# Two GNN layers on 4096 nodes: layer 0 from block sums of h by mask matmuls, lists and gathers only for edges that share a block

## The chip, the cores and the metric

The kernel runs on one core of a Trainium2 chip. The metric is the device time of one execution in microseconds (us); lower is better. Fourteen executions of the kernel before gave a median of 809.99 us, from 802.71 to 822.25 us. The engines are named as in the profile: PE (TensorE matmuls), PEld (TensorE weight loads, which overlap PE), DVE (VectorE), ACT (ScalarE), POOL (GpSimd), SP (SyncE, which here only issues transfers).

## What is computed

`x` is 4096 x 64 and `adj` a 4096 x 4096 matrix of zeros and ones, one entry in 512 set. Two layers follow each other, cut here to what matters:

```python
def logmap(x, y):                      # Poincare ball, c = 1
    sub = mobius_add(-x, y)            # a fraction in x, y and their dot products
    return 2 / lam(x) * arctanh(clip(norm(sub))) * sub / norm(sub)

h = relu(layernorm(x))
w = adj / deg                          # deg: row sums of adj
agg = einsum('ij,ijc->ic', w, logmap(h[:, None], h[None, :]))
x = x + expmap(0, agg @ W0 + b0)       # layer 0

h = relu(layernorm(x))
support = h @ W1
rank = cumsum(adj, axis=1); deg = rank[:, -1:]; k = minimum(deg, 100)
pos = rank - (deg - k)
w = adj * where(pos > 0, 0.5 ** (k - pos), 0)
x = x + w @ support + b1               # layer 1
```

Layer 0 weighs each edge (i, j) by a function of the squared distance of h_i and h_j, so it needs both rows for each edge. Layer 1 weighs the n-th edge of a row, counted from the right, by 2^-n.

## The kernel before

**Blocks.** The 4096 rows are 32 row blocks of 128 (NB = 32). Four quarters q hold eight row blocks each (QB = 8). The 4096 columns are 32 column blocks of 128. `load` (L814) brings a quarter of a row block, 128 x 1024 f32 or 512 KB, into a tile `a_sb` (three buffers), transposes it on PE by eight 128 x 128 matmuls (L821), and ACT writes it as an 8-bit mask into `masks[q]` (L823), which stays on the chip.

**Layer 0.** Each row has some eight edges. `pack` (L831) multiplies each 128 x 128 mask by an 8-column matrix `pk` (L845), so that every row gets 256 numbers, each of which encodes 16 columns. `search` (L858) takes the 24 largest of them with MAX8 and MATCH_REPLACE8. The first eight become lists of edges of the row itself (`ell_lists`, ELL = 8). What is over goes through `tail_split`, `tail_first` and `tail_second` (L889 to L994): edges of eight rows, then of a whole row block, are merged through DRAM tables `tl_d` and `ta_d` into lists that any row may own (TB = 2 a row block and partition), with the owner's number in `tail_r`. This happens once for each quarter. `gather` (L1006) fetches one h row for each partition with one indirect DMA of POOL: 256 for the row's own lists and 64 for the merged ones, 320 in all. `tail_rows` (L1022) makes one-hot matrices on POOL (L1031) and, by matmuls, the owners' rows. `differ`, `weigh`, `total` and `total_tail` (L1052 to L1145) compute differences, weights and sums on DVE and ACT. They run in 16 units of two row blocks; units 4 to 15 have some merged lists too. The sums are `st["y", q]`, from a pool of three buffers.

**Between the layers.** `middle` (L1163) finishes layer 0 for a group of row blocks and makes the support rows and their differences, split in three bf16 parts (`sup`).

**Layer 1.** `suffix` (L1254) and `ranks` (L1264) turn the masks into the powers of two. `collect` (L1288) multiplies them with `sup`: 33 blocks for each of 32 row blocks, 128 x 192 matmuls, in five sums (`sums`, L811), each added to `acc` by DVE (L1304, L1308).

**Order.** The program is written as a plan: `at(when, fn, ...)` gives each step a time in us, `EARLY` (L806) moves most steps but not the loads by 20 or 30 us ahead, and the result is a priority. A scheduler in the compiler orders each engine's queue from the priorities and its own estimates, and the engines run their queues in that order. The plan's lines for the lists are

```python
t = loaded(q * QB + QB - 1) + 6.0
at(t, tail_split, q)
at(t + 12.0, tail_first, q)
at(t + 20.0, tail_second, q)
```

If a list overflows, a flag is set and a slow second program (`dense_path`) runs after this one.

Of the kernel before, what the change touches and what calls it, by code (L numbers as in the profile page):

```python
# [11 lines left out]
F32 = mybir.dt.float32  # L12
# [7 lines left out]
P = 128  # L20
# [29 lines left out]
QB = 8  # L50
GRP = 16
CAND = 24
ELL = 8
EXTRA = 8
RUN = 8
TAILW = CAND - ELL + EXTRA
SUB = 40
REST = 64
TB = 2
MAXT = 3  # L60
# [484 lines left out]
def kernel(  # L545
# [37 lines left out]
    NSL = 2 * ELL + MAXT * TB  # L583
# [9 lines left out]
    hp_d = dram.tile([N, 3 * DT], BF16, name="hp_d")  # L593
# [7 lines left out]
    with ExitStack() as fast:  # L601
# [46 lines left out]
        pk = const.tile([P, GB], BF16, name="pk")  # L648
        nc.vector.tensor_scalar(pk, gm, pw_i.bitcast(F32), None, ALU.mult)
        gn = const.tile([1, NG], BF16, name="gn")  # L650
# [4 lines left out]

        row_b = const.tile([P, 1], F32, name="row_b")
# [3 lines left out]
        full = const.tile([P, NQ, 6], F32, name="full")  # L660
# [5 lines left out]
        ell_v = const.tile([P, NB, ELL], F32, name="ell_v")  # L666
        ell_i = const.tile([P, NB, ELL], I32, name="ell_i")
# [72 lines left out]
        nc.vector.tensor_copy(gn, gn_i)  # L740
# [44 lines left out]
        hp = masks[NQ - 2].bitcast(BF16).rearrange("p b c -> p (b c)")[:, 0 : NB * 3 * DT]  # L785
        hp = hp.rearrange("p (b n c) -> p b n c", n=3, c=DT)
        for n in range(3):
            nc.vector.tensor_copy(hp[:, :, n, :], tab)
            if n < 2:
                nc.vector.tensor_tensor(tab, tab, hp[:, :, n, :], ALU.subtract)  # L790
        nc.sync.dma_start(out=by_rows(hp_d), in_=hp.rearrange("p b n c -> p b (n c)"))

        gp = fast.enter_context(tc.tile_pool(name="gp", bufs=2))
        blk = fast.enter_context(tc.tile_pool(name="blk", bufs=1))
        blk2 = fast.enter_context(tc.tile_pool(name="blk2", bufs=2))
        yp = fast.enter_context(tc.tile_pool(name="yp", bufs=3))
# [3 lines left out]
        ps_w = fast.enter_context(tc.tile_pool(name="ps_w", bufs=1, space=PSUM))  # L800
        ps_t = fast.enter_context(tc.tile_pool(name="ps_t", bufs=1, space=PSUM))
        ps_o = fast.enter_context(tc.tile_pool(name="ps_o", bufs=1, space=PSUM))
        ps_s = fast.enter_context(tc.tile_pool(name="ps_s", bufs=1, space=PSUM))
        ps_m = fast.enter_context(tc.tile_pool(name="ps_m", bufs=1, space=PSUM))

        EARLY = {"middle":30,"search":30,"fetch_words":30,"tail_rows":30,"differ":30,"weigh":30,"total":30,"total_tail":30,"ell_lists":30,"tail_split":20,"tail_first":20,"tail_second":20,"gather":30,"fetch":30}  # L806
# [4 lines left out]
        sums = [range(0, 8), range(8, 16), range(16, 24), range(25, 30), (24, 30, 31, None)]  # L811
# [19 lines left out]
        def pack(rb, n):  # L831

            q, b = divmod(rb, QB)
            if n == 0 and rb % 2 == 0:
                st["words", rb // 2] = ps_w.tile([P, 2, NG], F32, name="words")
                nc.tensor.matmul(
                    st["words", rb // 2].rearrange("p k g -> p (k g)"),
                    lhsT=ones_r,
                    rhs=gn.unsqueeze(1).to_broadcast([1, 2, NG]),
                    start=True,  # L840
                    stop=True,
                )
            words = st["words", rb // 2]
            for j in range(RUN * n, RUN * n + RUN):
                nc.tensor.matmul(  # L845
                    words[:, rb % 2, bass.ts(j, GB)],
                    lhsT=masks[q][:, j, bass.ts(b, P)],
                    rhs=pk,
                    start=False,
                    stop=True,  # L850
                    skip_group_check=True,
                )

        def fetch_words(rb):
            st["wsb", rb // 2] = lst.tile([P, 2, NG], F32, name="wsb")
            nc.scalar.copy(st["wsb", rb // 2], st["words", rb // 2])  # L856

        def search(rb):  # L858
# [4 lines left out]
            src = st["wsb", rb // 2][:, rb % 2, :]  # L863
# [8 lines left out]
        def ell_lists(rb, nb):  # L872

            q, b = divmod(rb, QB)
            w = st["cand", q][:, b : b + nb, 0:ELL]
            r2 = slice(rb, rb + nb)
            ci = lst.tile([P, 4, ELL], I32, name="ci4")[:, 0:nb]
            e = lst.tile([P, 4, ELL], I32, name="e4")[:, 0:nb]
            kk = lst.tile([P, 4, ELL], F32, name="kk4")[:, 0:nb]
            t = lst.tile([P, 4, ELL], F32, name="t4")[:, 0:nb]  # L880
            nc.vector.tensor_copy(ci, w)
            nc.vector.tensor_scalar(ci, ci, NG - 1, None, ALU.bitwise_and)
            nc.vector.tensor_scalar(e, w.bitcast(I32), 23, None, ALU.logical_shift_right)
            nc.vector.tensor_scalar(kk, e, -135.0, float(NG), ALU.add, ALU.mult)
            nc.vector.scalar_tensor_tensor(t, kk, 1.0, ci, ALU.add, ALU.add)
            nc.vector.scalar_tensor_tensor(ell_v[:, r2], kk, 0.0, t, ALU.is_ge, ALU.mult)
            nc.vector.tensor_scalar(ell_i[:, r2], ell_v[:, r2], -1.0, 0.0, ALU.add, ALU.max)

        def tail_split(q):  # L889

            cand = st["cand", q]
# [559 lines left out]
```

## Time and profile before

| | |
|---|---|
| median of 14 runs | 809.99 us |
| the profiled execution | 811.75 us, its span 810.0 us |
| PE / PEld busy | 391.7 / 322.7 us |
| DVE busy | 486.0 us in 1635 instructions |
| ACT busy | 237.8 us |
| POOL busy | 394.8 us in 396 instructions |
| HBM read | 84.12 MB |
| granted TensorE clock, mean | 0.681 |

Busy is the time in which an engine had at least one instruction under way. A group's line has, after the count, its busy time, the mean of one instruction in ns, and the idle time of the engine just before such instructions with what ended it; "issue" there is time in which the engine waited for nothing that the profile shows. The granted clock is the share of TensorE's clock that the throttle gave, 1.0 being full. "PE a_ps L821 x8" is a stretch of eight instructions on that engine, writing that tile, of that line of the program.

### The profile page before, as it was taken

The numbers are of one execution on the slowest core, as the hardware profiler recorded it, in microseconds if no ns is written. First come the engines' busy times: TensorE is split into PE (matmuls) and PEld (weight loads), VectorE is DVE, ScalarE is ACT, GpSimd is POOL, SyncE is SP. The second block draws the span as 40 slices with busy tenths as digits, with TensorE's granted clock in tenths as the row PEclk, the third lists the DMA queues.
The fourth block names the chain that finished last, engine by engine and source line by source line (L and its number), as shares of the span: only waits on it lengthen the run. The fifth ranks groups of instructions, "written<-read, shape, count | busy, mean of one in ns | idle before, by whom it ended". The sixth has DMA issues, their size and how long they took to land.

```text
span 810.0 us, 10724 instructions
## 1 busy us (share of the span) xinstructions
PE 391.7 (48%) x3768; PEld 322.7 (40%) x3768; DVE 486.0 (60%) x1635; ACT 237.8 (29%) x335; POOL 394.8 (49%) x396
## 2 busy tenths in 40 slices
PE   4751227662753734212445548045136646468395
PEld 3640215451542522111235448033126545368284
DVE  5552139953984756775363336089936437569696
ACT  4640227752761614101211225025020102112100
POOL 0057472734187373277875642743858670741000
PEclk9999999755575555555556757555555959579598
DMA  7893447984884752011113448340211210100001
GB/s 243 273 347 104 116 137 240 294 252 123 261 258 130 246 162 58 18 31 30 32 29 93 101 124 258 67 105 13 34 22 32 31 22 12 26 13 3 0 2 56
DMA packets 49617, 89.11 MB, mean 110 GB/s; under 512 B 23571, under 2 KB 26899, under 8 KB 49299
## 3 DMA queue, kind: packets, MB, share of 16 engines
q1 hardware_dynamic: 32786, 74.93, 28.6%
q0 software_dynamic: 10240, 10.67, 8.9%
q10 hardware_dynamic: 6528, 2.75, 1.4%
q8 instruction: 31, 0.51, 0.3%
q14 instruction: 32, 0.25, 0.1%
HBM read 84.12 MB, written 4.19 MB: 109 GB/s over the span
## 4 chain that ended last, share of the span: by engine, by line
DVE 20%; PE 18%; another core or an unknown queue 16%; DMA 15%; issue 11%; POOL 11%; ACT 6%; SPq 1%; ACTq 0%; DVEq 0%; POOLq 0%
DMA a_sb<-in_adj 12%; POOL g L1014 8%; PE a_ps L1296 7%; PE a_ps L821 6%; ACT mask L823 3%; DVE red L1304 3%; POOL oh L1031 2%; DVE mask L1258 2%; PE words L1158 2%; DVE d L1089 1%; DVE acc L1308 1%; DVE d L1055 1%; PE sel L1124 1%; PE words L845 1%
## 5 line engine op out<-in xcount | busy, mean ns | idle before, releaser
L1014 POOL DMA_INDIRECT g<-tab_d,ell_i x256 | 278.5, 1088 | 288.6 <-issue 71.9
L823 ACT ACTIVATE mask<-a_ps 128x1024 fp8e5<-128x1024 bf16 x128 | 129.6, 1024 | 229.8 <-remote 116.8
L821 PE MATMUL a_ps<-ident_b,a_sb 128*128 128x128 bf16 x1024 | 129.3, 300 | 68.5 <-DMA a_sb<-in_adj 48.5
L821 PEld LDWEIGHTS <-a_sb 128*128 128x128 bf16 x1024 | 102.7, 162 | 83.4 <-DMA a_sb<-in_adj 61.6
L1296 PE MATMUL a_ps<-sup,mask 128*128 128x192 bf16 x1024 | 110.5, 267 | 36.0 <-issue 19.3
L1296 PEld LDWEIGHTS <-mask 128*128 128x128 fp8e5 x1024 | 97.5, 107 | 44.5 <-issue 41.4
L845 PE MATMUL words<-pk,mask 128*128 128x8 bf16 x1024 | 49.1, 171 | 112.0 <-ACT mask L823 77.3
L845 PEld LDWEIGHTS <-mask 128*128 128x128 fp8e5 x1024 | 43.2, 107 | 142.1 <-ACT mask L823 84.3
L1304 DVE TENSOR_REDUCE red<-a_ps 128x128 f32<-128x384 f32 x80 | 44.4, 555 | 70.1 <-remote 49.1
L1014 POOL DMA_INDIRECT g<-tab_d,tail_i x64 | 63.2, 987 | 18.4 <-issue 18.2
L1031 POOL TENSOR_SCALAR oh<-row,tail_r 128x128 bf16<-128x128 bf16 x64 | 51.3, 816 | 29.8 <-DVE r L1130 29.5
L1258 DVE TENSOR_TENSOR mask<-mask 128x512 int16<-128x512 int16 x112 | 43.1, 417 | 32.6 <-PE a_ps L821 19.8
L866 DVE MAX8 cand<-wsb 128x8 f32<-128x256 f32 x96 | 36.4, 413 | 33.5 <-ACT wsb L856 25.3
L1124 PE MATMUL sel<-d,mr 128*128 128x65 f32 x128 | 28.4, 392 | 52.1 <-issue 31.3
L1124 PEld LDWEIGHTS sel<-d,mr 128*128 128x128 f32 x128 | 26.9, 306 | 55.2 <-issue 51.0
L1089 DVE TENSOR_REDUCE d<-g 128x22 f32<-128x1408 f32 (+2 forms) x16 | 23.7, 1481 | 27.9 <-ACT g L1077 26.9
L1284 DVE TENSOR_TENSOR mask<-base,mask 128x4096 int16<-128x4096 int16 x16 | 36.5, 2280 | 5.0 <-ACT base L1280 5.0
L1036 PE MATMUL mi<-ident_b,oh 128*128 128x128 bf16 x64 | 13.7, 271 | 50.0 <-POOL oh L1031 37.8
L1154 PE MATMUL o<-ext,y 128*64 128x128 f32 x64 | 15.6, 384 | 40.6 <-DVE y L696 19.6
L1158 PE MATMUL words<-w_sb,a_sb 64*128 64x64 f32 x128 | 28.4, 388 | 10.0 <-ACT a_sb L1155 6.7
L1158 PEld LDWEIGHTS words<-w_sb,a_sb 64*128 64x128 f32 x128 | 25.3, 290 | 15.8 <-ACT a_sb L1155 10.2
L1155 ACT COPY a_sb<-o 64x512 f32<-64x512 f32 (+1 forms) x18 | 9.6, 532 | 74.1 <-PE o L1154 56.6
(310 smaller groups left out, 600.9 us busy)
## 6 DMA issues: line engine op xcount, KB each, us to landing
a_sb<-in_adj SPq DMA_DIRECT2D x128, 512.0 KB
g<-tab_d,ell_i POOLq DMA_INDIRECT x256
hp_d<-mask SPq DMA_DIRECT2D x1, 1560.0 KB
hr<-hp_d ACTq DMA_DIRECT2D x8, 146.2 KB
tab_d<-mask SPq DMA_DIRECT2D x1, 1040.0 KB
mask<-in_x SPq DMA_DIRECT2D x1, 1024.0 KB
hi<-tab_d ACTq DMA_DIRECT2D x16, 64.0 KB
g<-tab_d,tail_i POOLq DMA_INDIRECT x64
```

Of the source, the lines that this page charges most:

```text
L821: nc.tensor.transpose(a_ps[:, l, :], upper[:, l, :], ident_b)
L823: nc.scalar.activation(masks[q][:, bass.ts(n, RUN), bass.ts(b, P)], a_ps, AF.Copy, scale=2.0**-ONE_SHIFT, saturate=False,)
L845: nc.tensor.matmul(words[:, rb % 2, bass.ts(j, GB)], lhsT=masks[q][:, j, bass.ts(b, P)], rhs=pk, start=False, stop=True, skip_group_check= ...
L866: nc.vector.max(out=top, in_=src)
L1014: nc.gpsimd.indirect_dma_start(out=g[:, k, :], out_offset=None, in_=tab_d, in_offset=bass.IndirectOffsetOnAxis(ap=i, axis=0),)
L1031: nc.gpsimd.tensor_scalar(oh[:, k, :], row128, row[:, k : k + 1], None, ALU.is_equal)
L1124: nc.tensor.matmul(ag[:, k // TB, :], lhsT=mr[:, k, :], rhs=d[:, E2 + k, :], start=(k % TB == 0), stop=(k % TB == TB - 1),)
L1158: nc.tensor.matmul(sp[:, k, :], lhsT=ht[:, bass.ts(k, P)], rhs=w_sb, start=True, stop=True)
L1258: nc.vector.tensor_tensor(w[:, l, :], w[:, l, :], w[:, l + 1, :], ALU.add)
L1284: nc.vector.tensor_tensor(w, base.bitcast(I16).unsqueeze(1).to_broadcast([P, RUN, QR // 2]), w, ALU.subtract)
L1296: nc.tensor.matmul(o[:, k, :], lhsT=final if b is None else masks[p][:, b, rows], rhs=st["sup", c][:, j, :], start=(j == 0), stop=(j == nb ...
L1304: nc.vector.tensor_reduce(red, o.rearrange("p k (n c) -> p k c n", n=3), AX.X, ALU.add)
```

## The change

Layer 0 no longer lists every edge. Two column blocks of 128 make one "entry" of 256 columns (NE = 16 entries a row). `pack` now multiplies each mask by 12 columns (the eight of before, a count, and three parts of a scalar of the row) and, by three matmuls of 64 columns, by the three bf16 parts of h, summed over an entry in PSUM. Where a row has exactly one edge in an entry the sum is that edge's h; `differ`, `square`, `weigh` and `total` take all 16 entries of each row. Entries with two or more edges get weight zero (`entries`), and only their words are kept for `search`, which now takes 16; these edges alone go through the merged lists, TB = 4 a row block and partition, so 128 gathers, and `tail_rows` and `total_tail` work by row block, with the one-hot matrices made on DVE and not on POOL. The product with the weights in `total` is on POOL. The three parts of h stay on the chip (`hp`, in a constant tile that later holds `sup`). In layer 1 the first three sums become one of 24 blocks, and the support rows go through DRAM (`sup_d`, `differences`). `ranks` works on halves. The PSUM tiles are dealt out anew, the pool of `y` has two buffers and that of `D`, the differences of a row block, three. `EARLY` is empty, and the plan has new times. The units are 20: 16 of two row blocks, of which unit n >= 4 also has the merged lists of row blocks 2(n-4) and 2(n-4)+1, and four that have lists alone.

```diff
-CAND = 24
-ELL = 8
+CAND = 16
...
-SUB = 40
+PAIR = 2
+SIDE = 12
+SUB = 56
+DEAL = 8
-TB = 2
+TB = 4
...
-        gp = fast.enter_context(tc.tile_pool(name="gp", bufs=2))
+        gp = fast.enter_context(tc.tile_pool(name="gp", bufs=1))
+        dp = fast.enter_context(tc.tile_pool(name="dp", bufs=3))
+        sqp = fast.enter_context(tc.tile_pool(name="sqp", bufs=1))
-        yp = fast.enter_context(tc.tile_pool(name="yp", bufs=3))
+        yp = fast.enter_context(tc.tile_pool(name="yp", bufs=2))
+        ps_g = fast.enter_context(tc.tile_pool(name="ps_g", bufs=2, space=PSUM))
...
-        sums = [range(0, 8), range(8, 16), range(16, 24), range(25, 30), (24, 30, 31, None)]
+        sums = [range(0, 24), range(25, 30), (24, 30, 31, None)]
...
             for j in range(RUN * n, RUN * n + RUN):
+                at = masks[q][:, j, bass.ts(b, P)]
                 nc.tensor.matmul(
-                    words[:, rb % 2, bass.ts(j, GB)],
-                    lhsT=masks[q][:, j, bass.ts(b, P)],
-                    rhs=pk,
+                    st["words", rb][:, j, :], lhsT=at, rhs=side[:, j, :],
...
+                for t in range(3):
+                    nc.tensor.matmul(
+                        st["g", rb, hf][:, j // PAIR - hf * HE, :], lhsT=at, rhs=hp[:, j, t, 1:DT],
...
+        def entries(u):
+            nc.vector.tensor_tensor(cf, sv[:, :, 0, 0], sv[:, :, 1, 0], ALU.add)
+            nc.vector.tensor_reduce(we, sv[:, :, :, 1:], AX.XY, ALU.add)
...
+            nc.vector.scalar_tensor_tensor(we, cf, 1.5, we, ALU.is_lt, ALU.mult)
+            nc.vector.tensor_reduce(deg[:, rb : rb + 2], cnt, AX.X, ALU.add)
...
+            nc.vector.tensor_tensor(words, words, cols(mf, PAIR * GB), ALU.mult)
...
         def tail_second(q):
-            for k in range(4):
-                nc.sync.dma_start(
+            for k in range(DEAL):
+                for o in range(2):
+                    nc.sync.dma_start(out=dst[o], in_=src[o, DEAL - 1 - k if o else k])
...
-        def tail_rows(u):
-                nc.gpsimd.tensor_scalar(
+        def tail_rows(u, b):
+            for k in range(TB):
+                nc.vector.tensor_scalar(
                     oh[:, k, :], row128, tail_r[:, rb, k : k + 1], None, ALU.is_equal
...
+        def differ(u, b, hf):
+            if hf == 0:
+                u["D", b] = dp.tile([P, NE, D], F32, name="D")
             nc.vector.tensor_tensor(
+                u["D", b][:, hf * HE : (hf + 1) * HE, :],
+                st["g", rb, hf],
+                u["hi"][:, b, :].unsqueeze(1).to_broadcast([P, HE, D]),
                 ALU.subtract,
...
+        def square(u, b):
+                sq = sqp.tile([P, NE, D], F32, name="sq")
+                nc.scalar.activation(sq, u["D", b], AF.Square)
+                nc.vector.tensor_reduce(u["d2"][:, b * NE : (b + 1) * NE], sq, AX.X, ALU.add)
...
         def total(u):
+            for k in range(2):
+                dk = u["D", k]
+                nc.gpsimd.tensor_tensor(dk, dk, cols(r[:, k * NE : (k + 1) * NE]), ALU.mult)
+                nc.vector.tensor_reduce(
+                    y[:, b + k, 0:D], dk.rearrange("p e c -> p c e"), AX.X, ALU.add
...
+        def total_tail(u, b):
+            for k in range(TB):
+                nc.vector.tensor_scalar(
+                    mr[:, k, :], row128, tail_r[:, rb, k : k + 1], r[:, k : k + 1],
+                    ALU.is_equal, ALU.mult,
...
+        def differences(c, s):
+            if c == 0:
+                nc.sync.dma_start(out=dd[:, 1 : n + 1, :], in_=own)
+                nc.sync.dma_start(out=dd[:, 0:1, :], in_=prev[:, 0:1, :])
...
-        T0, TLOAD = 6.0, 8.4
+        T0, TLOAD = 6.0, 9.5
...
+        units = [{"rb": 2 * n, "tail": None} for n in range(NB // 2)]
+        units += [{"rb": None, "tail": None} for n in range(QB // 2)]
+        for n in range(NB // 2):
+            units[n + QB // 2]["tail"] = 2 * n
...
+            t = loaded(q * QB + QB - 1) + 5.0
             at(t, tail_split, q)
-            at(t + 12.0, tail_first, q)
-            at(t + 20.0, tail_second, q)
+            at(t + 8.0, tail_first, q)
+            at(t + 16.0, tail_second, q)
```

## The prediction

> **What bounds the kernel now.** I read the page first, then the busy time by stretches, then the groups of instructions, the timeline and the chain of waits. The page:
>
> ```profile
> PE 391.7 (48%) x3768; PEld 322.7 (40%) x3768; DVE 486.0 (60%) x1635; ACT 237.8 (29%) x335; POOL 394.8 (49%) x396
> ...
> DVE 20%; PE 18%; another core or an unknown queue 16%; DMA 15%; issue 11%; POOL 11%; ACT 6%; SPq 1%; ACTq 0%; DVEq 0%; POOLq 0%
> DMA a_sb<-in_adj 12%; POOL g L1014 8%; PE a_ps L1296 7%; PE a_ps L821 6%; ACT mask L823 3%; DVE red L1304 3%; POOL oh L1031 2%; DVE mask L1258 2%; PE words L1158 2%; DVE d L1089 1%; DVE acc L1308 1%; DVE d L1055 1%; PE sel L1124 1%; PE word
> ```
>
> No engine is full, and the chain that ends last changes engine all the time: its largest share is 20%. So I look at the stretches (stretch, its length, then busy time of each engine with the number of instructions, granted clock, share and rate of the transfers):
>
> ```profile
> 125.00:150.00 25.00, 19.18 (x228) 14.25 (x226) 23.98 (x89) 21.44 (x27) 11.77 (x10) 1.00 0.86 273
> ...
> 289.00:437.00 148.00, 44.53 (x249) 31.90 (x250) 85.81 (x282) 27.88 (x48) 98.23 (x100) 0.50 0.20 40
> ...
> 526.00:740.00 214.00, 111.95 (x892) 94.87 (x892) 142.46 (x465) 41.21 (x73) 116.76 (x118) 0.63 0.16 29
> ...
> 740.00:810.00 70.00, 44.32 (x402) 37.70 (x401) 52.28 (x187) 7.62 (x26) 0.00 (x0) 0.82 0.05 17
> ```
>
> From 125 to 150 us DVE is full, while the loads run at 273 GB/s. From 289 to 437 the loads nearly stop (40 GB/s) and POOL has 98 of 148 us. Most of it is gathers:
>
> ```profile
> L1014 POOL DMA_INDIRECT g<-tab_d,ell_i x256 | 278.5, 1088 | 288.6 <-issue 71.9 <-DVE u L1090 50.5 <-DVE d L1089 50.0
> ...
> L1014 POOL DMA_INDIRECT g<-tab_d,tail_i x64 | 63.2, 987 | 18.4 <-issue 18.2 <-DVE red L1304 0.2
> ...
> L1031 POOL TENSOR_SCALAR oh<-row,tail_r 128x128 bf16<-128x128 bf16 x64 | 51.3, 816 | 29.8 <-DVE r L1130 29.5
> ...
> L845 PEld LDWEIGHTS <-mask 128*128 128x128 fp8e5 x1024 | 43.2, 107 | 142.1 <-ACT mask L823 84.3 <-issue 56.1 <-DVE mask L1258 0.6
> ...
> L1089 DVE TENSOR_REDUCE d<-g 128x16 f32<-128x1024 f32 x4 | 4.9, 1214 | 24.9 <-ACT g L1077 24.9
> ...
> L1207 DVE TENSOR_TENSOR y<-y,th_n 128x512 f32<-128x512 f32 x3 | 2.1, 697 | 0.0
> ...
> L933 DVE TENSOR_SCALAR tl<-scr,row_b 128x128 f32<-128x128 f32 x4 | 1.1, 274 | 0.0
> ```
>
> The gathers take 278.5 + 63.2 us, and 90.1 us of issue lie before them (71.9 + 18.2), so that one gather costs about 1.35 us of POOL's queue. With L1031 that queue has some 485 us to do, 72% of the time from 62 us, when the table it gathers from is written, to 740. It is as heavy as DVE's, which can start at once. After 740 POOL is idle and 70 us of sums and writes remain. The least that this order could take is 62 + 485 + 70 = 617 us; the other 193 of the span are waits of POOL for DVE and back.
>
> **What goes.** 256 gathers of 1.088 us and their issue: 350 us off POOL. 64 more merged ones come: 64 x (0.987 + 0.28) = +81. The one-hot matrices (L1031) leave: -51. The products in `total` come, 32 of 128 x 1024. No row has one. Bounds: DVE's own 128 x 1040 product took 1.24 us; L1031 scaled from 128 to 1024 elements is 8 x 0.816 = 6.5. L1031's time is partly a fixed cost, so I take 3 us: +96. POOL falls from 485 to about 261 us, at most 373, and is no longer the heaviest by either.
>
> L1031 shows how unsteady POOL's arithmetic is: the same instruction takes 0.590 to 4.417 us by the list of that line. The Trainium skill (GPSIMD Engine Reference, Engine selection) says that elementwise work with two inputs belongs on VectorE, since GpSimd is about twice as slow; by it the product would be near 2 x 1.24 = 2.5 us (an estimate), which speaks against putting it there, but the sum below doesn't hang on it.
>
> **What comes on DVE.** Adding count x mean of all DVE groups gives 582 us, of which 486 are busy time, as instructions overlap at their ends: factor 0.835. Out: the row lists' differences, squares, products and sums (L1055 to L1138) 91; one third of the MAX8 and half of the replacements, 29; `ell_lists` 13; the merged lists' parts 22; narrower list work 8; 32 of 80 pairs L1304 and L1308 (0.555 + 0.289), 27. Together 190. In: 64 subtractions of 128 x 512 at 0.697 (L1207), 45; 64 reductions of 1024 at 1.214 (L1089), 78; squares of the merged lists 13; `entries` 16 x 2.3 (ten small operations and one of 512), 37; 256 one-hot operations of 128 x 128 at 0.27 (L933), 69; their differences and sums 24; four more units of `weigh` and small ones, 23. Together 289. Net +99, times 0.835: DVE goes from 486 to about 569 us.
>
> **What comes on PE.** 3072 matmuls of 64 columns, each with its own weight load. The timeline has the two neighbours, of 8 columns and of 192:
>
> ```profile
> 244.47 1.28 PE L845 MATMUL words<-pk,mask 128*128 128x8 bf16 x42
> ```
>
> ```profile
> 634.37 5.86 PE L1296 MATMUL a_ps<-sup,mask 128*128 128x192 bf16 x48 [1.89 <-DVE red L1304]
> ```
>
> ```profile
> 732.43 2.80 PE L1296 MATMUL a_ps<-sup,mask 128*128 128x192 bf16 x32
> ```
>
> 42 of 8 columns in 1.28 us are 30.5 ns each; of 192 columns 48 in 5.86 (122 ns, half clock for the most part) and 32 in 2.80 (87 ns). So 64 columns cost between 30 and 122 ns; in proportion to the columns 48 to 58. I take 52: 160 us, bounds 94 to 375. PE's 392 becomes about 560 with the 192 more matmuls of the merged lists.
>
> The group L845 PEld above says 107 ns for a weight load, and the Trainium skill (TensorE: Matmul & The Clock Gate, LDWEIGHTS) gives the same, 128 columns / 1.2 GHz. If loads could not overlap, that rule would make the new matmuls 3072 x 0.107 = 329 us (an estimate) instead of 160. The 30.5 ns pairs show that loads do overlap each other here, so the rule isn't in the sum.
>
> ACT goes from 238 to about 290 (32 squares of 1024 at 1.06 and smaller copies), below the others.
>
> **So the heaviest queue gets heavier:** POOL's 485 is replaced by DVE's 569 and PE's 560, side by side.
>
> **The sum by stages.** *Start:* `pack` now needs the parts of h; the last of them (L788) starts at 52.8 us, so 55 (loads and transposes go on meanwhile). *Sixteen units of two row blocks.* PE, from these pieces of the chain:
>
> ```profile
> 17.29 1.09 PE a_ps L821 x8
> ...
> 414.08 3.64 PE sel L1124 x12
> ...
> 552.60 1.19 PE sel L1042 x18
> ```
>
> Eight loads x 1.09 = 8.7; 64 x 0.0305 = 2.0; 192 x 0.052 = 10.0; merged lists: 8 x 0.136 + 24 x 1.19/18 + 8 x 3.64/12 = 5.1; ranks (32 x 0.573 + 24 x 0.547)/16 = 2.0: together 27.8. DVE: differences 2.8, two reductions 4.9, search 2.6, `entries` 2.3, weights 2.8, merged lists 6.7, list work 4.9, suffix and ranks 5.0 = 32.0, x 0.835 = 26.7. The larger: 16 x 27.8 = 445, if nothing waits. *Waits for lists.* From the first step of `tail_split` to the last of `tail_second`:
>
> ```profile
> L894 DVE TENSOR_REDUCE full<-cand x4: 146/151/159, 132.0 to 551.0; 128x1 f32<-128x8 f32 x4
> ```
>
> ```profile
> L994 DVE CAST tail_r<-li x4: 155/167/174, 234.7 to 619.0; 128x16 f32<-128x16 int32 x4
> ```
>
> The first is at 132.0, the last at 551.0; tail_r is written first at 234.7 and last at 619.0. With the two between (213.6 to 339.9, 291.0 to 363.1) the lists of the four quarters took 103, 126, 72 and 68 us. Before, POOL had row lists to gather meanwhile. Now unit 4q + 4 cannot be weighed before quarter q's lists and gathers; three `D` buffers hold one unit and a half, then `differ` waits, then `ps_g`, then PE's queue with the next transposes, and the SP queue with the next loads. I take 87 for the first three quarters (between 103 and 72), and 8 more because `tail_second` issues 16 transfers instead of 4, each 0.7 us behind the other on the SP queue (L969 in the timeline). After the lists come eight gathers, 10 us. Covered are the unit under way (27.8), the lists' own DVE time, already counted (16), and one `middle` (14): 95 + 10 - 58 = 47, three times: 141. *Finish:* `entries` and search 5; lists 68 + 8 = 76; four units with gathers alone, 8 x 1.27 + some 10 of chain each, 80; from the last gather to the end 73, as before (736.8, the last group's `middle`, to 810). Together 234. Sums over 24 blocks run on PE in that time: 768 x 87 ns = 67 us, which this finish hides.
>
> 55 + 445 + 141 + 234 = **875 us** of span. The profiled execution before had 811.75 with a span of 810.0, within 0.3% of the median, so I say **873 us**, 8% slower. What I cost at nothing: `differences` and the trip of `sup_d` through DRAM (some 10 us, hidden by the four last units; without them it is on the path) and the new setup (hidden by the first loads).
>
> **Rivals.**
> 1. *Lists run fast because nobody is before them* (faster). While the units wait, DVE has little else. Quarter 2 took 23 us from its write at 340.2 to 363.1; with 12 for the split and the 8 more that is 43, below the 58 of cover: no waits, finish 201, sum 701. Halfway, with 57: 3 x 9 + 215 + 500 = 742. For: where everything waits for a list, its steps meet no other work in DVE's queue. Against: DVE has 83 us more to do, and its queue's order is fixed beforehand. With L for the lists' time the sum is 500 + 3 (L - 48) + L + 158 = 514 + 4 L from 48 up, so the sign turns at 74 us. I give it 742 and 0.35.
> 2. *PE takes the bound* (much slower). At the upper bound of 122 ns a new matmul: 16 x 192 x 0.070 = 215 more, sum 1090; halfway 980. For: granted clock 0.50 over most of the loading. Against: more PE work should raise it, as at 125 us. 0.10.
> 3. *No difference:* lists at 73 to 75 us, 806 to 814: 0.04.
> 4. *The change doesn't do what it says:* an overflowing list would start the second program, far beyond 1000 us. I counted on the inputs: 13,114 of 32,916 edges share a block; the fullest of the merged lists has 61 of 63 places, eight rows at most 46 of 55. So no overflow, and 13,114 fit in 128 x 128 places. Under 0.01.
>
> **How the numbers follow.** Forecast 0.51, with its own range 815 to 930 (lists at 75 to 105). Faster by over 0.5% (what a measurement of this kernel can tell, some 4 us): rival 1, 0.35. Within: 0.04. Slower: 0.51 + 0.10 = 0.61. The range leaves out a tenth at each end: of rival 1 all below 715, of rival 2 all above 980.
>
> **What would show it.** Right: DVE's busy time 550 to 590 and PE's 530 to 600; POOL under 300; new words matmuls at 45 to 60 ns; stops of the loads after row blocks 10, 18 and 26; lists of 75 us or more. Wrong: lists of 45 us and no stops (rival 1); PE full between 60 us and the last load (rival 2); POOL's products at 6 us on the chain of a unit (two of them between weights and sums).

## The result and the profile after

The changed kernel takes 917.68 us (median of 10 executions, 915.1 to 922.37) beside 810.13 us of the kernel before (47 executions): a ratio of 1.138, interval 1.135 to 1.142. The profiled execution took 918.78 us, its span 916.8. On the chip of the runs e10 to e12 below, called the second place here, the same two kernels take 866.83 and 712.17 us: a ratio of 1.217, interval 1.214 to 1.219. So the change makes the kernel slower in both places.

The page of the changed kernel, busy times and then the chain that ended last:

```profile
PE 538.5 (59%) x7230; PEld 466.7 (51%) x7230; DVE 639.5 (70%) x2005; ACT 288.7 (31%) x483; POOL 194.0 (21%) x172
...
DVE 35%; PE 27%; DMA 18%; issue 6%; SPq 5%; another core or an unknown queue 3%; ACT 2%; POOL 2%; DVEq 0%; ACTq 0%
DMA a_sb<-in_adj 14%; PE g L865 9%; PE a_ps L1326 8%; DVE mr L1160 6%; PE a_ps L837 5%; SPq L999 4%; DVE y L1145 4%; DVE mask L1288 3%; DVE mask L1312 3%; PE y L1166 2%; POOL g L1039 2%; DVE d L1100 2%; DVE red L1334 2%; DMA ta_d<-tac 1%
```

DVE and PE have both grown (486 to 640 us, 392 to 539), POOL has halved (395 to 194), and the span grew by 107 us. The chain still changes engine all the time; no engine is full on the average. The groups of instructions that the prediction had to price:

```profile
L865 PE MATMUL g<-hs,mask 128*128 128x64 bf16 x3072 | 128.9, 209 | 6.1 <-DVE D L1082 5.7 <-issue 0.2
...
L1160 DVE TENSOR_SCALAR mr<-row,tail_r,r 128x128 f32<-128x128 bf16 x128 | 70.0, 600 | 0.1
...
L1144 POOL TENSOR_TENSOR D<-D,r 128x1024 f32<-128x1024 f32 x32 | 62.0, 1961 | 256.6 <-DVE r L1133 153.4 <-DVE found L965 85.5 <-DVE kd L1209 17.7
...
L1145 DVE TENSOR_REDUCE y<-D 128x64 f32<-128x1024 f32 x32 | 60.4, 1891 | 3.6 <-POOL D L1144 3.6
...
L1100 DVE TENSOR_REDUCE d<-sq 128x16 f32<-128x1024 f32 x32 | 38.7, 1209 | 4.6 <-ACT sq L1099 4.6
...
L1053 DVE TENSOR_SCALAR oh<-row,tail_r 128x128 bf16<-128x128 bf16 x128 | 24.6, 268 | 18.3 <-PE x L1058 14.1 <-remote 2.5 <-issue 1.4
```

Three of them differ from the price. L1145, the sum over a row's 16 entries, takes 1.891 us, though it reads as many elements as L1100 at 1.209; it reads every 64th element, and writes 64 results where L1100 writes 16. L1160 takes 600 ns on the mean and not 270. L1144 takes 1.96 us and not 3. The stretches, cut at the ends of units 0, 3, 4, 7, 8, 11, 12, 15, 16 and 19 (the end of a unit is that of its last L1145 or L1171); columns as before:

```profile
82.20:168.30 86.10, 66.79 (x1075) 57.56 (x1072) 74.31 (x193) 54.95 (x83) 13.08 (x6) 0.66 0.71 226
168.30:254.80 86.50, 46.87 (x619) 40.36 (x620) 43.96 (x158) 34.77 (x47) 19.09 (x18) 0.56 0.60 173
254.80:360.20 105.40, 64.22 (x1008) 56.38 (x1006) 86.41 (x239) 44.96 (x71) 27.94 (x22) 0.66 0.42 114
360.20:446.30 86.10, 44.63 (x567) 38.14 (x565) 51.49 (x195) 25.25 (x45) 18.94 (x18) 0.56 0.37 96
446.30:544.40 98.10, 50.43 (x849) 42.77 (x847) 87.52 (x241) 25.79 (x49) 28.30 (x22) 0.64 0.08 10
...
620.50:702.70 82.20, 36.01 (x487) 28.70 (x484) 75.46 (x210) 21.97 (x40) 30.94 (x22) 0.62 0.09 14
702.70:763.70 61.00, 23.17 (x144) 18.98 (x144) 36.22 (x160) 8.79 (x21) 15.52 (x16) 0.56 0.16 24
763.70:864.30 100.60, 88.17 (x900) 82.46 (x901) 47.47 (x190) 12.44 (x33) 15.13 (x16) 0.86 0.05 7
864.30:916.80 52.50, 33.49 (x306) 28.74 (x305) 36.01 (x118) 2.63 (x10) 0.00 (x0) 0.83 0.07 23
```

In the plain stretches, where no list ends between the units, DVE is busy for 86% (units 1 to 3), 82% (units 5 to 7), 89% (units 9 to 11) and 92% (units 13 to 15) of the time. Over these twelve units that is 27.0 us of DVE a unit, and 18.1 us of PE, in 31.0 us. In the stretches of 86 us, in which one unit alone ends, DVE is at 51 and 60%: there the kernel waits. After unit 15 there are 61.0 us with PE at 38% and DVE at 59%, then the list-only units, in which the sums over 24 blocks fill PE.

The lists, first step and last step over the four quarters (min/median/max in ns, first and last start):

```profile
L928 DVE CAST sq<-cand x4: 208/213/220, 140.5 to 680.2; 128x128 int32<-128x128 f32 x4
```

```profile
L1025 DVE CAST tail_r<-li x4: 182/182/250, 205.8 to 737.2; 128x32 f32<-128x32 int32 x4
```

With the two between (332.0 to 400.0, 514.3 to 581.4) and the last step itself the lists take 66, 68, 67 and 57 us. What comes behind a list is in the timeline, here of the first boundary, where unit 4 ends at 254.8 (in brackets the idle time of the engine before the instruction and what ended it):

```profile
206.67 1.07 PE L837 MATMUL a_ps<-ident_b,a_sb 128*128 128x128 bf16 x8 [2.42 <-DMA a_sb<-in_adj]
...
209.65 0.63 PE L1058 MATMUL x<-ident_b,oh 128*128 128x128 bf16 x4
...
211.45 1.08 PE L837 MATMUL a_ps<-ident_b,a_sb 128*128 128x128 bf16 x8 [1.16 <-DMA a_sb<-in_adj]
...
212.32 0.87 PE L1064 MATMUL x<-hs,mt 128*128 128x65 bf16 x12
...
238.24 0.37 ACT L875 COPY swords<-words 128x256 f32<-128x256 f32 x1 [6.64 <-remote]
...
238.81 0.22 DVE L889 TENSOR_TENSOR cnt<-sums 128x32 f32<-128x32 f32 x1 [10.95 <-ACT sums L878]
...
243.09 4.10 DVE L1160 TENSOR_SCALAR mr<-row,tail_r,r 128x128 f32<-128x128 bf16 x3
...
243.09 3.75 POOL L1144 TENSOR_TENSOR D<-D,r 128x1024 f32<-128x1024 f32 x2 [6.56 <-DVE r L1133]
...
250.56 1.11 DVE L1160 TENSOR_SCALAR mr<-row,tail_r,r 128x128 f32<-128x128 bf16 x4
...
253.57 4.45 PE L865 MATMUL g<-hs,mask 128*128 128x64 bf16 x96
```

After the list's end at 206, PE does the transposes of the next loads, each behind its own load, and the matmuls of unit 4's merged lists in between. At 238 ACT has waited 6.6 us for something the profile can't name ("remote"), and DVE 11 us for ACT. Only then come the weights and the sums, in which two instructions of L1160 wait out the two POOL products beside them (three in 4.10 us); four later ones, with POOL done, take 1.11 us in all. The last line prices the new matmuls: 96 in 4.45 us, 46 ns each.

### The profile page after: what moved, and what is told of

It reads as the page before. It is cut to its first block, busy times and chain, and to the rows that moved or that the text cites. A ratio compares the mean times of both kernels' runs of the same rounds, so it can differ in the third digit from the quotient of the medians.

```text
span 916.8 us, 18034 instructions
## 1 busy us (share of the span) xinstructions
PE 538.5 (59%) x7230; PEld 466.7 (51%) x7230; DVE 639.5 (70%) x2005; ACT 288.7 (31%) x483; POOL 194.0 (21%) x172
## 4 chain that ended last, share of the span: by engine, by line
DVE 35%; PE 27%; DMA 18%; issue 6%; SPq 5%; another core or an unknown queue 3%; ACT 2%; POOL 2%; DVEq 0%; ACTq 0%
DMA a_sb<-in_adj 14%; PE g L865 9%; PE a_ps L1326 8%; DVE mr L1160 6%; PE a_ps L837 5%; SPq L999 4%; DVE y L1145 4%; DVE mask L1288 3%; DVE mask L1312 3%; PE y L1166 2%; POOL g L1039 2%; DVE d L1100 2%; DVE red L1334 2%; DMA ta_d<-tac 1%
## 5 line engine op out<-in xcount | busy, mean ns | idle before, releaser
L1039 POOL DMA_INDIRECT g<-tab_d,tail_i x128 | 130.1, 1016 | 367.3 <-ACT a_sb L1181 98.4
L837 PE MATMUL a_ps<-ident_b,a_sb 128*128 128x128 bf16 x1024 | 121.7, 290 | 111.2 <-DMA a_sb<-in_adj 105.0
L865 PE MATMUL g<-hs,mask 128*128 128x64 bf16 x3072 | 128.9, 209 | 6.1 <-DVE D L1082 5.7
L865 PEld LDWEIGHTS <-mask 128*128 128x128 fp8e5 x3072 | 126.8, 109 | 9.0 <-issue 8.5
L1326 PE MATMUL a_ps<-hs,mask 128*128 128x192 bf16 x1024 | 110.4, 266 | 20.9 <-DVE red L1334 13.3
L1144 POOL TENSOR_TENSOR D<-D,r 128x1024 f32<-128x1024 f32 x32 | 62.0, 1961 | 256.6 <-DVE r L1133 153.4
L1326 PEld LDWEIGHTS <-mask 128*128 128x128 fp8e5 x1024 | 96.8, 107 | 29.7 <-issue 27.1
L1166 PEld LDWEIGHTS y<-d,mr 128*128 128x128 f32 x256 | 57.7, 314 | 98.5 <-DVE mr L1160 88.5
L1166 PE MATMUL y<-d,mr 128*128 128x65 f32 x256 | 65.6, 412 | 68.6 <-DVE mr L1160 62.8
L1160 DVE TENSOR_SCALAR mr<-row,tail_r,r 128x128 f32<-128x128 bf16 x128 | 70.0, 600 | 0.1
L860 PEld LDWEIGHTS <-mask 128*128 128x128 fp8e5 x1024 | 37.3, 102 | 61.3 <-issue 60.9
L1145 DVE TENSOR_REDUCE y<-D 128x64 f32<-128x1024 f32 x32 | 60.4, 1891 | 3.6 <-POOL D L1144 3.6
L1312 DVE TENSOR_TENSOR mask<-base,mask 128x2048 int16<-128x2048 int16 x32 | 44.5, 1394 | 2.5 <-ACT base L1310 2.5
L1100 DVE TENSOR_REDUCE d<-sq 128x16 f32<-128x1024 f32 x32 | 38.7, 1209 | 4.6 <-ACT sq L1099 4.6
```

Source lines behind the costliest of these rows:

```text
L837: nc.tensor.transpose(a_ps[:, l, :], upper[:, l, :], ident_b)
L860: nc.tensor.matmul(st["words", rb][:, j, :], lhsT=at, rhs=side[:, j, :], start=False, stop=True, skip_group_check=True,)
L865: nc.tensor.matmul(st["g", rb, hf][:, j // PAIR - hf * HE, :], lhsT=at, rhs=hp[:, j, t, 1:DT], start=(j % PAIR == 0 and t == 0), stop=(j % ...
L1039: nc.gpsimd.indirect_dma_start(out=g[:, b * TB + t, :], out_offset=None, in_=tab_d, in_offset=bass.IndirectOffsetOnAxis(ap=tail_i[:, t0 + ...
L1144: nc.gpsimd.tensor_tensor(dk, dk, cols(r[:, k * NE : (k + 1) * NE]), ALU.mult)
L1145: nc.vector.tensor_reduce(y[:, b + k, 0:D], dk.rearrange("p e c -> p c e"), AX.X, ALU.add)
```

## Experiments

The runs e1 to e7 were made on two chips where the kernel before takes 808 to 812 us and are set against 917.68. The runs e8 and e9, on a third, and e10 to e12, on a fourth, were made where it takes 712 and are set against e10's 866.83. Stage sums, in us, from the ends of the units as above (a plain period is one unit that ends without a list before it; "lists" is from first to last step, "behind" from there to that unit's end, both for the first three quarters):

| | prediction | after | e10 (after, second place) | e1 | e11 | e12 |
|---|---|---|---|---|---|---|
| end of unit 0 | 82.8 | 82.2 | 84.4 | 90.3 | 83.9 | 80.5 |
| 12 plain periods | 333.6 | 371.8 | 352.0 | 397.1 | 354.1 | 355.7 |
| 3 boundary periods | 224.4 | 248.7 | 228.9 | 166.2 | 214.4 | 227.8 |
| after unit 15 | 234 | 214.1 | 196.6 | 199.1 | 199.0 | 193.9 |
| span | 875 | 916.8 | 861.9 | 852.7 | 851.4 | 857.9 |
| lists | 95 each | 66, 68, 67 | 62, 70, 67 | 91, 85, 76 | 63, 67, 65 | 64, 71, 60 |
| behind | 10 each | 49, 46, 39 | 42, 38, 34 | not gated | 40, 34, 34 | 58, 30, 30 |

**e1: nothing waits for a list.**

```diff
+        nc.gpsimd.iota(tail_i..., pattern=[[31, NB * TB]], base=0, channel_multiplier=1)
+        nc.vector.tensor_copy(tail_r..., part_i.to_broadcast([P, NB * TB]))
...
-            nc.vector.tensor_scalar(tail_i[:, bs], li, N - 1, None, ALU.bitwise_and)
+            nc.vector.tensor_scalar(li, li, N - 1, None, ALU.bitwise_and)
...
-            nc.vector.tensor_copy(tail_r[:, bs], li)
+            nc.vector.tensor_copy(li.bitcast(F32), li)
```

> The merged lists are made as before, but what gathers and one-hot matrices read (tail_i, tail_r) is filled with constants in the setup, so nothing waits for a list; the merged edges are then wrong ones, everything else is computed. Theory (the lists gate the units of the next quarter): the three long periods of 78 to 88 us between units at the quarters' boundaries shrink to about the others' 31, 161 us less, and the 37 us between unit 15 and the first list-only unit go too; 917 - 161 - 37 = 720 us. Rival (DVE's heavier queue of 640 us sets the time and the waits at the boundaries are only where its work piles up): the periods in between grow instead, 840 us or more. Rival (PE's new matmuls set it): the same, 840 or more, with PE full between the boundaries.

Measured 854.58 us: 63 less, far from the theory's 720 and in the band of both rivals, and as they had it the 12 plain periods grow, by 25. But the first boundary's wait is gone (86.5 to 37.3 us), and the second and third shrink (86.1 and 76.1 to 68.2 and 60.7). So the lists are a real gate; what came of it is less than half of the 161 us that the theory had put on the boundaries, and part of what they cost goes over to other waits. What holds unit 8 in their place, from the timeline of this run (the lines of this kernel are moved by 6):

```profile
356.33 11.12 SPq L1005 DMA_DIRECT2D tb_i<-ta_d  x16
...
370.95 1.08 PE L843 MATMUL a_ps<-ident_b,a_sb 128*128 128x128 bf16 x8 [9.16 <-DMA a_sb<-in_adj]
...
380.48 1.06 PE L1186 MATMUL y<-ext,y 128*64 128x128 f32 x4
...
391.52 0.22 DVE L1177 TENSOR_TENSOR y<-y 128x65 f32<-128x65 f32 x1 [11.42 <-PE y L1172]
...
393.46 3.77 DVE L1151 TENSOR_REDUCE y<-D 128x64 f32<-128x1024 f32 x2 [0.68 <-DMA sup_d<-y]
```

PE's transposes stand 9 us behind a load, while SP issues the 16 transfers of a list, and after them `middle` of the first group (L1186); DVE waits 11 us for the matmuls of unit 8's merged lists (L1172), which are behind both in PE's queue. Then unit 8's first sum into a new `y` waits 0.68 us more for the transfer that empties the old one into `sup_d`. The pool of `y` has two buffers, so the third quarter's sums need the first group to be through `middle`, whose own steps run on PE between the transposes.

**e2: one part of h.** Two of the three bf16 parts are left out of the block sums.

```diff
-                for t in range(3):
+                for t in range(1):
```

> Only the first of the three bf16 parts of h is summed over an entry: 2048 of the 3072 matmuls of 64 columns are left out (the sums are then less exact). They take 46 ns each in the profile, so PE has 94 us less to do. Theory (the lists gate the units; between the boundaries PE and DVE are about even): the 13 plain periods lose 2 to 3 us each, the boundaries nothing; 880 to 905 us. Rival (PE's matmuls are on the path everywhere): 16 times 5.9 us less, some 820 us.

Measured 900.37 us, in the band of the theory and far from the rival's 820. L865 falls from 128.9 to 56.3 us of busy time, but PE as a whole only from 538.5 to 489.3: with a third of the new matmuls the granted clock was 0.625 to 0.627 in all four runs, beside 0.671 to 0.688 in the changed kernel's, and the transposes went from 121.7 to 128.9 us. And the 17 us came at the boundaries (248.7 to 238.6) as much as in the plain periods (371.8 to 366.0), which isn't where the theory had put them. So two thirds of PE's new matmuls are worth 17 us of the 107, lower clock included; they aren't what makes the kernel slow.

**e3: total's product on DVE.**

```diff
-                nc.gpsimd.tensor_tensor(dk, dk, cols(r[:, k * NE : (k + 1) * NE]), ALU.mult)
+                nc.vector.tensor_tensor(dk, dk, cols(r[:, k * NE : (k + 1) * NE]), ALU.mult)
```

> The 32 products of D with the weights (128x1024) in total go from POOL to DVE. Theory (DVE's one-hot products mr are held up by POOL's product running beside them, 1.9 instead of 0.28 us): mr falls from a mean of 600 ns to below 300, 70 to some 36 us of busy time, while 32 x 1.24 = 40 us come onto DVE; DVE about 640 as now, and the time within 10 us of 917. Rival (no such interference, mr is slow for another reason): mr stays at 600 ns, DVE goes to 680 and the time to 940 or more. Rival (the way from the weights over POOL and back to DVE is on each unit's path): 20 units times some 2 us less, 880.

Measured 916.63 us. The two groups:

```profile
L1144 DVE TENSOR_TENSOR D<-D,r 128x1024 f32<-128x1024 f32 x32 | 37.8, 1222 | 0.3
...
L1160 DVE TENSOR_SCALAR mr<-row,tail_r,r 128x128 f32<-128x128 bf16 x128 | 35.6, 347 | 0.1
```

L1160 halves with POOL's product out of the way, and the product costs on DVE about what that gives back (DVE 639.5 to 630.9 us). Both parts of the theory hold: the interference is real, and moving the product is worth nothing. L1145 stays at 1.896 us, so its price is its own and not POOL's doing. In the changed kernel the spread of L1160 shows the same:

```profile
L1160 DVE TENSOR_SCALAR mr<-row,tail_r,r x128: 330/340/4448, 243.1 to 862.4; 128x128 f32<-128x128 bf16 x128
```

The 109 of them that met no product took 0.33 to 0.50 us, the 19 that did 1.87 us or more. The profile of the kernel before has the like in the other direction:

```profile
318.42 8.79 POOL L1031 TENSOR_SCALAR oh<-row,tail_r 128x128 bf16<-128x128 bf16 x3 [11.85 <-DVE r L1130]
318.94 2.26 DVE L1284 TENSOR_TENSOR mask<-base,mask 128x4096 int16<-128x4096 int16 x1
321.13 1.22 DVE L1134 TENSOR_TENSOR d<-d,r 128x1040 f32<-128x1040 f32 x1
...
323.88 2.27 DVE L1284 TENSOR_TENSOR mask<-base,mask 128x4096 int16<-128x4096 int16 x1
```

Three of L1031, whose median is 0.602 us, take 8.79 in all beside such operations of DVE on two tensors. The prediction read that spread as POOL's own unsteadiness and had no term for the interference; no run tests this direction.

**e4: list and unit steps 30 us earlier in the plan.** `EARLY` gets 30 for them, and for `middle`.

> All steps of the lists and of the units get a plan time 30 us earlier (loads, matmuls and layer 1 keep theirs), as the kernel before had it for its steps; nothing else changes. Theory (the lists gate the units): the lists' steps stand earlier in DVE's queue, they take 50 instead of 65 us, and the three waits and the finish shorten by 15 each; 860 us. Rival (DVE's work in all sets it, or the queue's order is near the best already): within 15 us of 917.

Measured 927.6 us: the rival. The first three lists take 64 to 68 us as before, and the plain periods grow to 391.8. So standing 30 us earlier in the plan doesn't help; no other place was tried.

**e5: no products and no sums in total.**

```diff
-                nc.gpsimd.tensor_tensor(dk, dk, cols(r[...]), ALU.mult)
-                nc.vector.tensor_reduce(y[:, b + k, 0:D], dk.rearrange("p e c -> p c e"), AX.X, ALU.add)
+                nc.vector.tensor_copy(y[:, b + k, 0:D], dk[:, 0, :])
```

> In total the 32 products of D with the weights on POOL and the 32 sums over the 16 entries on DVE are left out; a copy of 128x64 stands in their place, so layer 0's sums are not the true ones for edges alone in their entry. That takes 62 us from POOL and, from DVE, 60 us of sums less 7 of copies and some 35 us by which POOL's products hold up the products mr: DVE 640 to some 552. Theory A (between the boundaries DVE's queue sets the pace, at the boundaries the lists): plain periods fall by some 5 us each, 12 of them, and the units at the boundaries and in the finish by 2 to 3: 840 us, boundaries still 80 long. Theory B (PE's queue sets the plain periods): within 20 us of 917. Theory C (only the lists and the steps behind them count): the same within 20.

Measured 841.32 us, DVE 540.1 us busy. Theory A's number came, its picture only in part: the second and third boundary fell too, from 86.1 and 76.1 to 63.4 and 62.4 us. And e9 and e11 speak against A as it was put. The run also takes away more than work: the copy needs no weights, so units 0 to 3 are through with it at 57.8 to 87.3 us and not at 82.2 to 168.3, and the `D` buffers come free that much sooner. What part of the 76 us is DVE's work and what part is this, the run can't tell, and its plain periods can't be compared with the others.

**e6: e1 and e5 together.**

> Both cuts together: the lists' results are replaced by constants as in the run with free lists (855 us), and total's products and sums are left out. DVE has some 540 us to do. Theory A (with the lists' waits gone DVE's own work sets the time; 628 of 853 us busy there): 88 us less than 855, that is 767, below the kernel before. Theory B (in that run PE's order with the transposes of the loads sets the pace): 835 or more.

Measured 811.77 us, between the two. Of 63 and 76 us, 106 came: the two costs lie partly on top of each other. With no wait for a list and without 122 us of product and sum the kernel is still no faster than the kernel before (811.61 there).

**e7, e9 and e11: mr on ACT.** In e7 with two buffers of `a_sb`, in e9 and e11 (the same program twice) with three.

```diff
-                nc.vector.tensor_scalar(mr[:, k, :], row128, tail_r[:, rb, k : k + 1], r[:, k : k + 1], ALU.is_equal, ALU.mult)
+                nc.scalar.activation(mr[:, k, :], u["oh", b][:, k, :], AF.Copy, scale=r[:, k : k + 1])
```

> The 128 products mr of total_tail are made by ACT, from the one-hot matrices of tail_rows, which are kept for it, instead of by DVE from the numbers; a_sb has two buffers and not three, for the room. DVE loses 70 us (640 to 570), ACT gains some 128 x 0.3 = 38. Theory A (DVE's queue sets the plain periods): 16 units with lists, each some 4 us shorter: 850 to 865. Rival (DVE is not on the path where mr runs, or ACT's queue with the masks' copies is late instead): 905 or more.

> As the run with the products mr on ACT (913 us), but with three buffers of a_sb as in the changed kernel; mt takes the buffer of mr for the room instead. Theory A (DVE's queue sets the plain periods, and the run with two buffers lost to the loads what DVE won): 855 to 870. Rival (70 us of DVE's work less are worth nothing, since these products are not on the path; the 76 us of the run without total's sums came from the way from the weights over POOL's product to the sum): 905 or more.

> mr on ACT with three buffers of a_sb once more, beside the changed kernel. Theory A (DVE's queue sets the plain periods): 40 us or more below the changed kernel in the same place. Rival (not on the path): within 12 us of it.

e7 measured 912.96 us, in the rival's band, but decides nothing: with two buffers the transposes of row block 30 start at 524.7 us and not at 392.7. e9 measured 850.57 and e11 855.99, so 16 and 11 us below e10. The bands of e9 were meant for the first place and can't be read here; e11 is the rival. The plain periods didn't shorten (352.0 to 354.1), so 35 us less busy time on DVE (632.7 to 597.7) is worth little there. Why not 70 less, the groups of e11 show:

```profile
L1053 DVE TENSOR_SCALAR oh<-row,tail_r 128x128 bf16<-128x128 bf16 x128 | 44.8, 429 | 11.7 <-ACT mr L1160 11.6
...
L1160 ACT ACTIVATE mr<-oh,r 128x128 f32<-128x128 bf16 x128 | 40.8, 391 | 36.5 <-PE y L1163 25.4 <-DVE r L1133 11.1
```

and its timeline, where DVE's `oh` of the next unit meets the two products:

```profile
456.27 4.91 DVE L1053 TENSOR_SCALAR oh<-row,tail_r 128x128 bf16<-128x128 bf16 x4 [0.24 <-ACT mr L1160]
...
457.37 3.76 POOL L1144 TENSOR_TENSOR D<-D,r 128x1024 f32<-128x1024 f32 x2
```

The held-up instruction is now L1053: from 262 ns in e10 to 429. Four that take 0.73 us alone take 4.91. The wait has moved to the next instruction of that kind in the queue. In e12, with the product on DVE, the longest L1053 takes 0.444 us.

**e8: the lists' transfers from POOL's queue.** The four `dma_start` of `tail_split`, `tail_first` and `tail_second` go from `nc.sync` to `nc.gpsimd`; the product of total is on DVE as in e3.

> The 19 transfers of each list (tl out, ti in, ta out, 16 times tb_i in) are issued from POOL's queue instead of SP's, where the loads of adj are issued; and the products of total are on DVE, as in the run with them there (917 us), so that POOL has only gathers and lists to issue. Theory (the list's transfers hold up SP's queue, with it the next loads, and PE's transposes of those loads stand ahead of the matmuls of the unit that waits for the list: 47, 44, 37 us from the list's end to that unit's end): these 47, 44, 37 us become 25 or less, and a period at a boundary 65 instead of 86; 850 us. Rival (the loads come late for want of buffers and of PE's time, not for SP's queue): within 15 us of 917.

Measured 871.23 us, beside 866.83: the rival's result, no gain. The times behind the lists became 60, 34 and 35 us, against 42, 38 and 34, and PE still waits 109.7 us for loads (118.8 in e10), so SP's queue alone isn't what makes them late. But the parts moved: the second and third boundary period fell from 79.3 and 71.1 to 68.5 and 68.6 us, and the first grew from 78.7 to 98.4, where DVE's `oh` waits up to 19.95 us for PE. e12 beside e11 shows the same signs (70.6 and 67.9 to 66.2 and 63.7, and 75.9 to 97.9). So the transfers on SP's queue may cost something at the later boundaries; what moved the first, no run shows.

**e10: the changed kernel where the kernel before takes 712 us.**

> The changed kernel itself, as the scale for the last runs: beside the two runs with POOL's queue and with mr on ACT the kernel before took 712 us and not 810, so their times can't be set against 917. In those two traces nothing waited for another core or an unknown queue, where the changed kernel's DVE, ACT and SP had 76 us of such waits and the kernel before's 337. If these waits are what differs, then where the kernel before takes 712 the changed kernel takes 850 to 890, and where it takes 810, 917 again; a ratio of 1.14 in both places would speak against it.

866.83 us, as expected, and the kernel before 712.17. The page's first line and one of its waits (total, times, longest):

```profile
PE 523.5 (61%) x7230; PEld 455.6 (53%) x7230; DVE 632.7 (73%) x2005; ACT 288.8 (34%) x483; POOL 194.7 (23%) x172
```

```profile
DVE cnt L889 <- ACT sums L878: 18.4, 10, 3.8
```

The same waits of the changed kernel in the first place:

```profile
DVE cnt L889 <- ACT sums L878: 38.9, 9, 10.9
```

```profile
ACT swords L875 <- remote: 26.8, 5, 9.2
```

Nothing in e10 waits for an unknown queue; most other waits are of about the same size in both, but DVE's wait for ACT halves, since it had stood behind ACT's. Busy times hardly differ. So the 55 us between the spans (916.8 and 861.9) go with these waits. In the profile of the kernel before they were larger: 131 us on SP, 139 on ACT, 67 on DVE, and that kernel takes 98 us more in the first place than in the second. What the waits are stays open, and so whether the chip makes the difference; the kernel before wasn't profiled in the second place.

**e12: all three.** mr on ACT, the product on DVE, the lists' transfers from POOL's queue.

> mr on ACT, the products of total on DVE, and the lists' transfers from POOL's queue, all three together; the result is the full one. If the transfers of the lists hold up the loads on SP's queue, it is 25 us or more below the run with mr on ACT alone; if not, within 10 us of it. To beat the kernel before where that takes 810 it must save 107 us on the changed kernel; from the two parts I expect some 80, so 835 there.

Measured 862.87 us, 4 below e10 and 7 above e11, where some 80 had been expected from the parts. No version of the full kernel here beats the kernel before.

## Why the prediction was right, and where its terms were off

The direction holds, and of the reason this part: POOL was relieved as priced (194 us busy, L1144 cheaper than taken), and what replaced it was more work on DVE and PE plus waits at the quarters' boundaries, of which e1 shows the lists to be one. That DVE's heavier queue is the rest is argued and not shown. The forecast of 875 us of span was 42 short of 916.8, and 13 above the 861.9 of e10. It was built of instruction and list times alone, and set against a measured 811.75 us in which three engines together waited 337 us for an unknown queue. The chain of the kernel before had 16% on "another core or an unknown queue", and the sum had no term for that; where such waits exist, they go with 55 us more for the changed kernel and 98 for the kernel before. So in the second place the change costs 155 us and not 63. Of the signs that the prediction named, POOL's and PE's busy time and the price of a new matmul came; DVE at 550 to 590 us (639.5), lists of 75 us or more (57 to 70) and stops of the loads didn't. Term by term, against e10, which has none of the unknown waits:

- **Start** (55 + one unit = 82.8): 84.4, right.
- **Plain periods** (27.8 each, set by PE): 29.3. The size came, but not from PE: it is busy for 18.1 us of a plain period of the changed kernel and DVE for 27.0. Two thirds of the new matmuls less (e2) shorten a period by 0.5 us, 35 us less on DVE (e11) by nothing, so neither engine alone sets it; what does stays open, and that 29.3 lies so near 27.8 is luck. PE's price was right, 46 ns against 52 for a new matmul. The Trainium skill (TensorE: Matmul & The Clock Gate, LDWEIGHTS) puts a weight load at its columns over 1.2, so 107 ns for 128 (an estimate). The 4.45 us for 96 pairs show that this isn't the pace of such a stream. DVE's total was too little: 639.5 us busy and not 569. The mis-sized steps are "256 one-hot operations at 0.27" (L1160 took 600 ns, 70 us and not 35) and "64 reductions at 1.214" (32 of them took 1.891, 22 us more). e3 shows the cause of the first: without the product beside it, 347 ns. What the missed 70 us cost is only known for half of them: e11 took 35 away and gained 11.
- **Waits for lists** (47 each): (228.9 - 3 x 29.3)/3 = 47.0. The size is right by two errors that cancel. A list took 66.5 us and not 95: the guess from the older lists plus 8 for the 16 transfers was too high. Behind it came 38 us and not 10: the step "after the lists come eight gathers, 10 us" left out the one-hot matrices, transposes and owners' rows of the unit, behind the loads' transposes in PE's queue, and its weights and sums. 66.5 + 38 - 58 = 46.5. Rival 1's formula, 514 + 4L, would have given 780 at L = 66.5 and a faster kernel; it fell with the same 10 us. The forecast hangs on them too: with the right time for a list and its own 10 us behind it, it would have named the wrong direction. That it came out is luck in this term.
- **Why the units wait**: e1 shows the lists as one gate of at least two; the others that its timeline shows, at the second boundary, are the loads' transposes and `middle` in PE's queue, and the two `y` buffers behind `middle`. The prediction had counted `middle` as cover for the wait; it is itself part of one. The loads didn't stop, as the prediction had it; they ran ahead, with the transposes of row block 30 at 392.7 us and its block sums only after 640. What stopped was `pack`.
- **Finish** (234): 196.6. After unit 15 the list needed 35 us more and not 81, the four units 109 and not 80 (most of it with PE full of the 24-block sums), the end 53 and not 73.

Rival 2 (PE takes the bound) is refuted by e2; that SP's queue makes up the wait, e8 and e12 speak against, with the later boundaries left open. Open is also which way e5's 76 us went: total's product and sums lie before the release of the `D` buffers that `differ` needs, and a run with more `D` buffers would test it; it wasn't tried. Part of the 76 us may also be fewer waits for the unknown queue.

## What to carry to other kernels

When work moves off a full queue, price what stands behind each new gate, up to the end of the unit that waits, and not only the gate: here the 38 us behind a list mattered as much as its 66. A share of a profile that belongs to no engine or tile (16% here) needs a term of its own in the sum, or a second place to measure. A ring cut from three buffers to two can be a new wait, and work counted as cover may be what the ring waits for. A sum that comes out right proves no term of it: check each against the profile, and the busy time of the engine that is said to set a stage against that stage's length.

## What the runs showed of the hardware

- A product of two tensors on POOL (128x1024, 1.96 us; 1.22 on DVE in e3) held up one-hot instructions on DVE, 1.9 us instead of 0.34, whole instruction by whole instruction, and when one kind was moved away the next kind waited in its place (L1053 in e11, 4.91 us for four). The f32 sums L1100 and L1145 that ran beside such a product took 1.21 and 1.88 to 1.92 us, as they did elsewhere. The Trainium skill (SBUF — State Buffer, SBUF: two separate sides) says that the port pair shared by the two is an exclusive lock for the whole instruction, and that the loser fully blocks; the 1.9 us beside 1.96 agree.
- A sum over 16 values that lie 64 elements apart, 64 results, took 1.89 us, one over 64 neighbours in as many elements, 16 results, 1.21, with POOL's product (changed kernel) or without (e3). Whether the step or the number of results makes the difference, no run shows.
- Told above: the granted clock that fell with less to do for PE (e2, 0.626 for 0.677), and the same kernels at 810 and 712, 917 and 867 us, the slower changed kernel with waits of which the profile doesn't name the source (e10).
